# A two-stage Mamba scan: one softplus sum moved to TensorE, B and C spread by DMA, half-size dt transfers, and five products in 32 on GpSimd

## The chip, the cores and the metric

One core of a Trainium2 chip runs the whole program. The metric is the device time of one execution in microseconds, the median of three. Engines are named as the profile names them: PE (TensorE matmul), PEld (its weight load), DVE (VectorE), ACT (ScalarE), POOL (GpSimd) and SP (SyncE, which issues all DMAs here).

## The reference

The input is x of 64 channels, 256 time steps and 128 frequencies. Layer 0 runs a bidirectional Mamba block along time (128 sequences of length 256), adds a linear map of it, then does the same along frequency (256 sequences of length 128). Layer 1 is a small convolutional LSTM over 32 windows. Only layer 0 is touched. Cut to what matters, one direction of one Mamba block is:

```python
dt, Bm, Cm = jnp.split(jnp.einsum('nld,ed->nle', x, x_proj_w), [4, 20], axis=-1)
dt = jax.nn.softplus(jnp.einsum('nlr,dr->nld', dt, dt_proj_w) + dt_proj_b)
A = -jnp.exp(A_log)                                   # (128 channels, 16 states)
def step(h, inp):
    dt_t, B_t, C_t, x_t = inp
    h = jnp.exp(dt_t[:, :, None] * A) * h + dt_t[:, :, None] * B_t[:, None, :] * x_t[:, :, None]
    return h, jnp.einsum('nds,ns->nd', h, C_t)
```

So each of 128 channels carries 16 states. Per token there is a decay exp(dt*A), an input dt*x*B, a recurrence over the sequence, and a sum over the states weighted by C.

## The kernel before, in words

**Tiling.** A *stage* is one of the two Mamba passes (time, then frequency). A stage is cut into NCH = 64 *chunks* of 512 tokens, and a chunk has two directions. The 128 channels times 16 states of a direction are 2048 rows, that is sixteen tiles of 128 rows; they are worked as eight *pairs* of two tiles (128 x 1024 elements). A pair is numbered S: 16 pairs a chunk (8 forward, 8 backward), 1024 a stage, 2048 in all. `where(S)` gives chunk, direction d and the pair's place (k, r).

**The work of a pair.** `inputs` (L428) multiplies dtx = dt*x by a 0/1 selection matrix on TensorE, which spreads 8 channels over 128 rows and leaves the pair `bx` in PSUM (three buffers). `decays` has ACT compute exp(A*rep) into one of four `dA` buffers (L450), where `rep` is dt spread over the states: it is written to DRAM by `dt_away` (L384) and read back with a broadcast by `spread_dt` (L403), 1 MB for two pairs, three buffers. `times_b` multiplies bx by B on DVE (L462). `recur` is the scan on DVE (L472), which writes `h` (five buffers). `outputs` multiplies h by C on POOL (L485). `add_up` sums the states of two pairs back onto channels on TensorE (L500, with a first matmul L493).

**Swapped pairs.** For S % 32 in (5, 21, 29) the product with B is done by POOL instead (L459). The bx tile is first copied from PSUM to a dA buffer by ACT (L444), POOL multiplies there, ACT puts the decays into the PSUM tile, and the scan reads its two operands in exchanged places.

**The head of a chunk.** What a chunk needs ahead of its pairs is listed in HEAD: each entry is a slot and a name. Slot n of chunk c is done in step S = 16*(c-1)+n, so slots 0 to 15 run beside the pairs of the chunk before and slots 16 and up beside the chunk's own pairs. `project_x`, `project_z` and `silus` make xs and zs. `softplus_a` and `softplus_b` do relu, exp, log and two corrections on ACT; `softplus_c` and `softplus_d` add the four parts with three adds on POOL (L374, L375, L378); `times_x` makes dtx on POOL (L389). `project_bc` makes B or C, already spread over 128 rows, with one matmul (L395, weights repeated eight times) and one ACT copy (L397): four a chunk. All these matmuls share a single PSUM buffer (`ps_mm`, tag "mm"), so each waits until ACT has read the one before.

**What sets the order.** The whole layer runs under a manual schedule: every engine executes its instructions in program order. `run` writes, in each step S: the product with B for S+1, the scan of S, the gate (at S % 8 = 2), the product with C for S-1, bx for S+2, the decays of S+2, the HEAD entries of this step, then add_up for S-2 at odd S, and the closing matmuls at S % 16 = 2 and 3. SP issues DMAs in the same order; an issue that must wait holds up those behind it. In the order of instructions each DMA also waits for the eighth DMA before it (eight completion semaphores in turn).

Of the kernel before, what the change touches and what calls it, by code (L numbers as in the profile page):

```python
# [36 lines left out]
P = 128  # L37
# [9 lines left out]
NTOK = 512  # L47
# [8 lines left out]
FH = F // 2  # L56
HALF = T // 2
NRING = 4
NH = 5
LAG = 2  # L60
SWAPPED = (5, 21, 29)
EXP_AND_LN = "natural_log_exp_and_others"
SILU = "silu_and_others"
EDGES = (0, 1, LF - 2, LF - 1)
# [2 lines left out]

HEAD = (
    (-12, "load"),
    (-7, "squares"),  # L70
    (-6, "means"),
    (-6, "rms"),
    (-6, "normalise"),
    (0, "project_x", 0),
    (1, "project_z", 0),
    (4, "project_x", 1),
    (5, "project_z", 1),
    (5, "silus"),
    (7, "softplus_a", 0),
    (7, "softplus_b", 0),  # L80
    (9, "softplus_c", 0),
    (9, "project_bc", 0, 1),
    (10, "softplus_d", 0),
    (10, "dt_away", 0),
    (11, "softplus_a", 1),
    (11, "spread_dt", 0, 0),
    (12, "times_x", 0),
    (12, "project_bc", 1, 1),
    (12, "project_bc", 0, 0),
    (12, "spread_dt", 0, 1),  # L90
    (13, "softplus_b", 1),
    (13, "project_bc", 1, 0),
    (14, "spread_dt", 0, 2),
    (15, "softplus_c", 1),
    (16, "softplus_d", 1),
    (16, "spread_dt", 0, 3),
    (17, "dt_away", 1),
    (18, "spread_dt", 1, 0),
    (20, "times_x", 1),
    (20, "spread_dt", 1, 1),  # L100
    (22, "spread_dt", 1, 2),
    (24, "spread_dt", 1, 3),
)


class Mamba:


    def __init__(self, ctx, tc, d):
        nc = tc.nc  # L110
        self.nc, self.tc = nc, tc
        cp = ctx.enter_context(tc.tile_pool(name="m_const", bufs=1))
# [47 lines left out]
        nc.scalar.activation(self.A, self.A, AF.Exp)  # L160
        nc.vector.tensor_scalar(self.A, self.A, -1.0, None, ALU.mult)

        self.G1, self.G2, self.Wz, self.Wdt, self.Wb, self.Wc, self.Dd, self.W2 = ([] for _ in range(8))
        self.W3, self.lin_b = [], []
        with tc.tile_pool(name="m_prep", bufs=2) as pp, tc.tile_pool(
            name="m_prep_ps", bufs=2, space=PSUM
        ) as ps:
            lins = []
            for i, n in enumerate(("tlin", "flin")):
                lin = pp.tile([C, 2, C], F32, name=n, tag=n, bufs=1)  # L170
                nc.sync.dma_start(out=lin, in_=d[n + "_w"].rearrange("(h i) o -> i h o", h=2))
# [12 lines left out]
            for i in range(4):
                win = pp.tile([C, 2 * P], F32, name="win", tag="win")
                nc.sync.dma_start(out=win, in_=d["in_proj"][i])
                cw = pp.tile([C, 4, P], F32, name="cw", tag="cw")
                nc.sync.dma_start(out=cw, in_=d["conv_w"][i].partition_broadcast(C))
                xpd = pp.tile([RANK, P], F32, name="xpd", tag="xpd")
                nc.sync.dma_start(out=xpd, in_=d["x_proj_dt"][i])  # L190
                dtw = pp.tile([RANK, P], F32, name="dtw", tag="dtw")
                nc.sync.dma_start(out=dtw, in_=d["dt_proj"][i])
                xbc = pp.tile([P, NBC], F32, name="xbc", tag="xbc")
                nc.sync.dma_start(out=xbc, in_=d["x_proj_bc"][i])
                ow = pp.tile([C, P], F32, name="ow", tag="ow")
# [20 lines left out]
                for h, keep in ((0, self.Wb), (1, self.Wc)):  # L216
                    w = cp.tile([P, NS, DL], F32, name=f"wbc{h}{i}", tag=f"wbc{h}{i}")
                    nc.vector.tensor_copy(
                        w, xbc[:, h * NS : (h + 1) * NS].unsqueeze(2).to_broadcast([P, NS, DL])
                    )  # L220
                    keep.append(w.rearrange("p s d -> p (s d)"))
# [12 lines left out]
class Stage:  # L234
# [142 lines left out]
    def softplus_d(self, ch, d):  # L377
        self.nc.gpsimd.tensor_add(self.at["dt", d], self.at["lw", d], self.at["dt", d])  # L378

    def dt_away(self, ch, d):  # L380

        there = self.dram.tile([32, 4, NTOK], F32, name="there", tag="there")
        for r in range(4):
            self.nc.sync.dma_start(out=there[:, r], in_=self.at["dt", d][32 * r : 32 * r + 32])  # L384
        self.at["there", ch, d] = there

    def times_x(self, ch, d):
# [1 line left out]
        self.nc.gpsimd.tensor_mul(dtx, self.at["dt", d], self.at["xs", ch, d])  # L389
        self.at["dtx", ch, d] = dtx  # L390

    def project_bc(self, ch, d, h):
        wt = (self.m.Wb, self.m.Wc)[h][2 * self.stage + d]
        pb = self.mm("pb")
        self.nc.tensor.matmul(pb, lhsT=wt, rhs=self.at["xs", ch, d], start=True, stop=True)  # L395
        t = self.wk.tile([P, NTOK], F32, name="bc", tag=f"bc{h}", bufs=3)
        self.nc.scalar.copy(t, pb)  # L397
        self.at["BC"[h], ch, d] = t

    def spread_dt(self, ch, d, k):  # L400
        t = self.wk.tile([P, 4, NTOK], F32, name="rep", tag="rep", bufs=3)
        there = self.at["there", ch, d]
        self.nc.sync.dma_start(  # L403
            out=t, in_=there[DL * k : DL * (k + 1)].unsqueeze(0).to_broadcast([NS, DL, 4, NTOK])
        )
        self.at["rep", ch, d, k] = t

    def head(self, ch):
        todo = {}
# [20 lines left out]

    def swapped(self, S):

        return S % 32 in SWAPPED

    def decays(self, S):
        nc, m, L = self.nc, self.m, self.L
        ch, d, k, r = self.where(S)
        i = 2 * self.stage + d
        first, live = (0, slice(1, L)) if d == 0 else (L - 1, slice(0, L - 1))
        dA = self.dA[S % NRING]  # L440
        rep = self.at["rep", ch, d, k]
        if self.swapped(S):
            bx = self.at["bx", S]
            nc.scalar.copy(dA.rearrange("p j n l -> p j (n l)"), bx)  # L444
# [701 lines left out]
```

## Time and profile before

| what | before |
|---|---|
| time, median of 3 | 7585.94 us (7581.3 to 7589.56) |
| span of the profiled run | 7581.6 us |
| first scan starts, stage 0 | 75.7 us |
| gap between the last scan of stage 0 and the first of stage 1 | 3453 to 3509.6 us |
| last scan ends (layer 1 follows) | 6890 us |
| bytes of the SP queue | 1203 MB |
| rep<-there transfers, there<-dt, unp<-xn | 1024 of 1024 KB, 1024 of 64 KB, 512 of 64 KB |

The page gives busy time by engine for the whole run, but the run has three regimes: two scan stages that look alike and layer 1, whose 690 us are bounded by matmuls and are not touched. So a question on the scan is asked of a stretch inside a stage, for instance 1000 to 3000 us. The timeline lists instructions with start and duration; as an instruction's end overlaps the start of the next one on the same engine by some 0.1 us, the cost of one is read as the distance between two starts. In the list of waits, an engine's idle time is put down to what ended it.

### The profile page before, as it was taken

To read this page: it belongs to the slowest core of one execution; us is meant where nothing else is said; L and a number is where in the kernel's file an instruction comes from. 1 tells how busy PE (TensorE), PEld (TensorE's weight loads), DVE (VectorE), ACT (ScalarE), POOL (GpSimd) and SP (SyncE) were. 2 spreads that over 40 slices of the span, in tenths; PEclk is the share of its full clock that TensorE was granted. 3 is DMA by queue.
4 is the path that set the end of the run, shared out by engine and by line. 5 is a ranking of instruction groups with operands and counts; after the bars stand their busy time and mean duration, and the time that the engine had idled before them with its cause. 6 is when DMAs were issued, how large, how long until landed. Compare 5 with 4: busy or idle time off the path is not lost.

```text
span 7581.6 us, 83087 instructions
## 1 busy us (share of the span) xinstructions
PE 6523.0 (86%) x24588; PEld 2179.7 (29%) x24588; DVE 7263.6 (96%) x5008; ACT 5568.8 (73%) x10188; POOL 6916.1 (91%) x3860
## 2 busy tenths in 40 slices
PE   6888888888888888887988888888888888888999
PEld 2222222222222222221222222222222222225887
DVE  6999999999999999997999999999999999996887
ACT  5778777777777877775787877878778787774333
POOL 6999999999999999996999999999999999995554
PEclk9999999999999999998999999999999999999999
DMA  5777877777777777775778777777777777772000
GB/s 131 175 178 175 183 174 177 174 174 182 176 181 174 174 182 177 180 173 124 184 182 186 171 176 172 171 181 172 178 173 171 179 171 179 172 172 77 15 15 17
DMA packets 276049, 1208.67 MB, mean 159 GB/s; under 512 B 46704, under 2 KB 104720, under 8 KB 144528
## 3 DMA queue, kind: packets, MB, share of 16 engines
q1 hardware_dynamic: 275600, 1203.35, 68.9%
q8 instruction: 200, 3.28, 0.2%
q14 instruction: 249, 2.04, 0.1%
HBM read 1094.12 MB, written 75.50 MB: 154 GB/s over the span
## 4 chain that ended last, share of the span: by engine, by line
PE 21%; ACT 10%; issue 9%; DVE 6%; DMA 5%; POOL 4%; SPq 0%; POOLq 0%; DVEq 0%; ACTq 0%
PE cv L911 6%; DVE h L472 5%; PE bx L428 4%; DMA rep<-there 4%; ACT dA L450 3%; POOL h L485 3%; PE y L500 2%; PE pb L395 2%; DVE bx L462 1%; PE y L493 1%; ACT L342 1%; PE pg L967 1%; PE px L322 1%; ACT L347 1%; PE both L1023 1%
## 5 line engine op out<-in xcount | busy, mean ns | idle before, releaser
L485 POOL TENSOR_TENSOR h<-h,bc 128x1024 f32<-128x1024 f32 x2048 | 4806.7, 2365 | 179.0 <-DVE h L472 167.7
L472 DVE TENSOR_TENSOR_SCAN h<-dA,bx 128x1024 f32<-128x1024 f32 x1856 | 4205.5, 2275 | 0.7 <-POOL e L374 0.7
L428 PE MATMUL bx<-dtx,sel 64*128 64x512 f32 x8192 | 2371.3, 654 | 755.2 <-DVE h L472 736.0
L450 ACT ACTIVATE dA<-rep,A 128x510 f32<-128x510 f32 (+1 forms) x3712 | 2461.6, 713 | 453.7 <-DMA rep<-there 439.9
L462 DVE TENSOR_TENSOR bx<-bx,bc 128x1024 f32<-128x1024 f32 x1856 | 2245.9, 1210 | 117.0 <-PE bx L428 116.0
L428 PEld LDWEIGHTS bx<-dtx,sel 64*128 64x128 f32 x8192 | 648.2, 189 | 2390.1 <-issue 1093.5
L500 PE MATMUL y<-h,fold 128*32 128x512 f32 x8192 | 1272.4, 638 | 25.9 <-POOL h L485 22.9
L395 PE MATMUL pb<-xs,wbc 128*128 128x512 f32 x1024 | 655.8, 726 | 119.8 <-ACT bc L397 112.8
L444 ACT COPY dA<-bx 128x1024 f32<-128x1024 f32 x192 | 194.4, 1012 | 474.7 <-PE bx L428 472.4
L500 PEld LDWEIGHTS y<-h,fold 128*32 128x32 f32 x8192 | 185.6, 111 | 969.8 <-issue 455.2
L459 POOL TENSOR_TENSOR dA<-dA,bc 128x1024 f32<-128x1024 f32 x192 | 453.5, 2362 | 5.6 <-ACT dA L444 5.6
L397 ACT COPY bc<-pb 128x512 f32<-128x512 f32 x512 | 294.4, 575 | 218.2 <-PE pb L395 218.2
L472 DVE TENSOR_TENSOR_SCAN h<-bx,dA 128x1024 f32<-128x1024 f32 x192 | 438.4, 2283 | 12.6 <-POOL dA L459 10.8
L374 POOL TENSOR_TENSOR e<-e,w 128x512 f32<-128x512 f32 x256 | 327.1, 1278 | 68.8 <-ACT w L369 68.4
L375 POOL TENSOR_TENSOR lw<-lw,e 128x512 f32<-128x512 f32 x256 | 326.0, 1273 | 20.1
L389 POOL TENSOR_TENSOR dtx<-dt,xs 128x512 f32<-128x512 f32 x256 | 327.4, 1279 | 0.0
L378 POOL TENSOR_TENSOR dt<-lw,dt 128x512 f32<-128x512 f32 x256 | 326.6, 1276 | 0.3
L395 PEld LDWEIGHTS pb<-xs,wbc 128*128 128x128 f32 x1024 | 166.9, 205 | 554.3 <-ACT bc L397 318.9
L322 PE MATMUL px<-unp,g 128*128 128x512 f32 x512 | 291.4, 650 | 31.3 <-ACT X L544 17.8
L324 ACT ACTIVATE xs<-px,cb 128x512 f32<-128x512 f32 x256 | 175.4, 685 | 175.9 <-PE px L323 173.9
L355 PE MATMUL pv<-xs,wdt 128*128 128x512 f32 x512 | 294.1, 657 | 12.0 <-ACT xs L346 9.9
L329 PE MATMUL pz<-unp,wz 64*128 64x512 f32 x512 | 271.0, 609 | 9.0 <-ACT xs L324 8.8
(187 smaller groups left out, 6983.0 us busy)
## 6 DMA issues: line engine op xcount, KB each, us to landing
rep<-there SPq DMA_DIRECT2D x1024, 1024.0 KB
there<-dt SPq DMA_DIRECT2D x1024, 64.0 KB
unp<-xn SPq DMA_DIRECT2D x512, 64.0 KB
u<-in_x SPq DMA_DIRECT2D x128, 64.0 KB
out<-y SPq DMA_DIRECT2D x32, 256.0 KB
w<-in_W_ih_f SPq DMA_DIRECT2D x10, 512.0 KB
w<-in_W_ih_b SPq DMA_DIRECT2D x10, 512.0 KB
cw<-in_conv_w SPq DMA_DIRECT2D x4, 128.0 KB
```

The costliest lines, as they stand in the source:

```text
L322: nc.tensor.matmul(self.seqs(px), lhsT=m.G1[i], rhs=self.unp[:, :, first : first + L], start=True, stop=False)
L374: self.nc.gpsimd.tensor_add(e, e, w)
L389: self.nc.gpsimd.tensor_mul(dtx, self.at["dt", d], self.at["xs", ch, d])
L395: self.nc.tensor.matmul(pb, lhsT=wt, rhs=self.at["xs", ch, d], start=True, stop=True)
L428: self.nc.tensor.matmul(bx[:, j], lhsT=self.m.sel[rows, r, k], rhs=dtx[rows], start=True, stop=True)
L450: nc.scalar.activation(dA[:, j, :, live], self.seqs(rep[:, r + 2 * j])[:, :, live], AF.Exp, scale=m.A[:, i, g : g + 1])
L459: self.nc.gpsimd.tensor_mul(bx, bx, b)
L462: self.nc.vector.tensor_mul(bx, bx, b)
L472: self.nc.vector.tensor_tensor_scan(h.rearrange("p j n -> p (j n)")[:, step], dA[:, step], bx[:, step], 0.0, ALU.mult, ALU.add,)
L485: self.nc.gpsimd.tensor_mul(h, h, self.at["C", ch, d].unsqueeze(1).to_broadcast([P, 2, NTOK]))
L500: nc.tensor.matmul(y[32 * r : 32 * r + 32], lhsT=m.fold[:, k], rhs=hs[r % 2][:, r // 2], start=False, stop=k == NK - 1, skip_group_check=True,
L911: self.nc.tensor.matmul(t[:, g, :, 0:n_out], lhsT=wts[s][:, gate * P : (gate + 1) * P], rhs=self.parts[n][:, :, s : s + n_out], start=s == ...
```

## The change

- **Softplus of direction 0**: the four parts (relu, exp, correction, log) are summed by four matmuls with the identity into PSUM and one ACT copy, instead of three POOL adds. Direction 1 keeps the POOL adds.
- **B and C**: one matmul a direction gives all 32 rows (16 of B, 16 of C), ACT copies 32 x 512, the tile goes to DRAM, and two DMAs read it back spread over 128 rows. The wide weights wb and wc go away.
- **rep**: a transfer carries the dt rows of one pair (512 KB) instead of two; seven buffers of half the size instead of three. `there` is laid out so that the two rows of a pair are adjacent.
- **Swapped pairs**: S % 32 in (5, 10, 15, 21, 26), five in two chunks instead of three.
- **HEAD** is rearranged to go with this.

It is for taking work off DVE (products with B) while giving POOL room for it.

```diff
-SWAPPED = (5, 21, 29)
+NREP = 7
+SWAPPED = (5, 10, 15, 21, 26)
...
-    (7, "softplus_a", 0),
-    (7, "softplus_b", 0),
-    (9, "softplus_c", 0),
-    (9, "project_bc", 0, 1),
-    (10, "softplus_d", 0),
+    (7, "project_bc", 0),
+    (8, "softplus_a", 0),
+    (8, "softplus_b", 0),
+    (9, "spread_bc", 0, 0),
+    (9, "spread_bc", 0, 1),
+    (10, "softplus_sum", 0),
     (10, "dt_away", 0),
+    (10, "spread_dt", 0, 0),
+    (11, "times_x", 0),
+    (12, "project_bc", 1),
+    (13, "softplus_a", 1),
+    (14, "softplus_b", 1),
+    (15, "spread_dt", 0, 2),
...
+    def softplus_sum(self, ch, d):
+        nc = self.nc
+        ps = self.mm("ps")
+        parts = [self.at[n, d] for n in ("dt", "e", "w", "lw")]
+        for n, t in enumerate(parts):
+            nc.tensor.matmul(ps, lhsT=self.m.ident, rhs=t, start=n == 0, stop=n == len(parts) - 1)
+        nc.scalar.copy(self.at["dt", d], ps)
...
-    def project_bc(self, ch, d, h):
-        wt = (self.m.Wb, self.m.Wc)[h][2 * self.stage + d]
-        pb = self.mm("pb")
-        self.nc.tensor.matmul(pb, lhsT=wt, rhs=self.at["xs", ch, d], start=True, stop=True)
-        t = self.wk.tile([P, NTOK], F32, name="bc", tag=f"bc{h}", bufs=3)
+    def project_bc(self, ch, d):
+        pb = self.mm("pb")[0:NBC]
+        self.nc.tensor.matmul(pb, lhsT=self.m.Wbc[2 * self.stage + d], rhs=self.at["xs", ch, d], start=True, stop=True)
+        t = self.wk.tile([NBC, NTOK], F32, name="bc", tag="bc")
         self.nc.scalar.copy(t, pb)
+        away = self.dram.tile([NBC, NTOK], F32, name="away", tag="away")
+        self.nc.sync.dma_start(out=away, in_=t)
+
+    def spread_bc(self, ch, d, h):
+        t = self.wk.tile([P, NTOK], F32, name="BC"[h], tag="BC"[h], bufs=3)
+        self.nc.sync.dma_start(
+            out=t, in_=away[NS * h : NS * (h + 1)].unsqueeze(1).to_broadcast([NS, DL, NTOK])
+        )
...
-        t = self.wk.tile([P, 4, NTOK], F32, name="rep", tag="rep", bufs=3)
+        t = self.wk.tile([P, 2, NTOK], F32, name="rep", tag="rep", bufs=NREP)
-            out=t, in_=there[DL * k : DL * (k + 1)].unsqueeze(0).to_broadcast([NS, DL, 4, NTOK])
+            out=t, in_=there[DL * k : DL * (k + 1), r].unsqueeze(0).to_broadcast([NS, DL, 2, NTOK])
```

More of the change, by code (lines that the diff above doesn't have):

```diff
@@ L69 @@
     (-12, "load"),
[L70 to L73, printed above, removed]
+    (-8, "squares"),
+    (-5, "means"),
+    (-5, "rms"),
+    (-4, "normalise"),
     (0, "project_x", 0),
@@ L78 @@
     (5, "silus"),
-    (7, "softplus_a", 0),
-    (7, "softplus_b", 0),
-    (9, "softplus_c", 0),
-    (9, "project_bc", 0, 1),
-    (10, "softplus_d", 0),
-    (10, "dt_away", 0),
[L85 to L89, printed above, removed]
-    (12, "spread_dt", 0, 1),
[L91 to L96, printed above, removed]
+    (7, "project_bc", 0),
[4 more added lines that the diff above has]
+    (10, "softplus_sum", 0),
+    (10, "dt_away", 0),
+    (10, "spread_dt", 0, 0),
+    (11, "times_x", 0),
+    (12, "project_bc", 1),
+    (12, "spread_dt", 0, 1),
+    (13, "softplus_a", 1),
+    (14, "softplus_b", 1),
+    (15, "spread_dt", 0, 2),
+    (15, "spread_dt", 0, 3),
+    (15, "spread_dt", 0, 4),
+    (15, "spread_dt", 0, 5),
+    (16, "softplus_c", 1),
+    (17, "softplus_d", 1),
+    (17, "spread_dt", 0, 6),
     (17, "dt_away", 1),
-    (18, "spread_dt", 1, 0),
+    (18, "spread_dt", 0, 7),
+    (20, "spread_dt", 1, 0),
+    (20, "spread_bc", 1, 0),
     (20, "times_x", 1),
+    (20, "spread_bc", 1, 1),
     (20, "spread_dt", 1, 1),
-    (22, "spread_dt", 1, 2),
-    (24, "spread_dt", 1, 3),
+    (23, "spread_dt", 1, 2),
+    (23, "spread_dt", 1, 3),
+    (23, "spread_dt", 1, 4),
+    (25, "spread_dt", 1, 5),
+    (26, "spread_dt", 1, 6),
+    (26, "spread_dt", 1, 7),
 )
@@ L161, in __init__ @@
         nc.vector.tensor_scalar(self.A, self.A, -1.0, None, ALU.mult)
-        self.G1, self.G2, self.Wz, self.Wdt, self.Wb, self.Wc, self.Dd, self.W2 = ([] for _ in range(8))
+        self.G1, self.G2, self.Wz, self.Wdt, self.Wbc, self.Dd, self.W2 = ([] for _ in range(7))
         self.W3, self.lin_b = [], []
@@ L192, in __init__ @@
                 nc.sync.dma_start(out=dtw, in_=d["dt_proj"][i])
-                xbc = pp.tile([P, NBC], F32, name="xbc", tag="xbc")
+                xbc = cp.tile([P, NBC], F32, name=f"xbc{i}", tag=f"xbc{i}")
                 nc.sync.dma_start(out=xbc, in_=d["x_proj_bc"][i])
+                self.Wbc.append(xbc)
                 ow = pp.tile([C, P], F32, name="ow", tag="ow")
@@ L214, in __init__ @@
                 self.Wdt.append(wdt)
[L216 to L221, printed above, removed]
                 dd = cp.tile([P, P], F32, name=f"dd{i}", tag=f"dd{i}")
@@ L378, in softplus_d @@
         self.nc.gpsimd.tensor_add(self.at["dt", d], self.at["lw", d], self.at["dt", d])
+    def softplus_sum(self, ch, d):
[5 more added lines that the diff above has]
+        nc.scalar.copy(self.at["dt", d], ps)
     def dt_away(self, ch, d):
-        there = self.dram.tile([32, 4, NTOK], F32, name="there", tag="there")
+        there = self.dram.tile([32, 2, 2, NTOK], F32, name="there", tag="there")
         for r in range(4):
-            self.nc.sync.dma_start(out=there[:, r], in_=self.at["dt", d][32 * r : 32 * r + 32])
+            self.nc.sync.dma_start(out=there[:, r % 2, r // 2], in_=self.at["dt", d][32 * r : 32 * r + 32])
         self.at["there", ch, d] = there
@@ L390, in times_x, with spread_dt @@
         self.at["dtx", ch, d] = dtx
-    def project_bc(self, ch, d, h):
-        wt = (self.m.Wb, self.m.Wc)[h][2 * self.stage + d]
-        pb = self.mm("pb")
-        self.nc.tensor.matmul(pb, lhsT=wt, rhs=self.at["xs", ch, d], start=True, stop=True)
-        t = self.wk.tile([P, NTOK], F32, name="bc", tag=f"bc{h}", bufs=3)
-        self.nc.scalar.copy(t, pb)
+    def project_bc(self, ch, d):
+        pb = self.mm("pb")[0:NBC]
+        self.nc.tensor.matmul(pb, lhsT=self.m.Wbc[2 * self.stage + d], rhs=self.at["xs", ch, d], start=True, stop=True)
+        t = self.wk.tile([NBC, NTOK], F32, name="bc", tag="bc")
+        self.nc.scalar.copy(t, pb)
+        away = self.dram.tile([NBC, NTOK], F32, name="away", tag="away")
+        self.nc.sync.dma_start(out=away, in_=t)
+        self.at["away", ch, d] = away
+    def spread_bc(self, ch, d, h):
+        t = self.wk.tile([P, NTOK], F32, name="BC"[h], tag="BC"[h], bufs=3)
+        away = self.at["away", ch, d]
+        self.nc.sync.dma_start(
+            out=t, in_=away[NS * h : NS * (h + 1)].unsqueeze(1).to_broadcast([NS, DL, NTOK])
+        )
         self.at["BC"[h], ch, d] = t
-    def spread_dt(self, ch, d, k):
-        t = self.wk.tile([P, 4, NTOK], F32, name="rep", tag="rep", bufs=3)
+    def spread_dt(self, ch, d, n):
+        k, r = divmod(n, 2)
+        t = self.wk.tile([P, 2, NTOK], F32, name="rep", tag="rep", bufs=NREP)
         there = self.at["there", ch, d]
         self.nc.sync.dma_start(
-            out=t, in_=there[DL * k : DL * (k + 1)].unsqueeze(0).to_broadcast([NS, DL, 4, NTOK])
+            out=t, in_=there[DL * k : DL * (k + 1), r].unsqueeze(0).to_broadcast([NS, DL, 2, NTOK])
         )
-        self.at["rep", ch, d, k] = t
+        self.at["rep", ch, d, n] = t
     def head(self, ch):
@@ L440, in decays @@
         dA = self.dA[S % NRING]
-        rep = self.at["rep", ch, d, k]
+        rep = self.at["rep", ch, d, 2 * k + r]
         if self.swapped(S):
@@ L450, in decays @@
             nc.scalar.activation(
-                dA[:, j, :, live], self.seqs(rep[:, r + 2 * j])[:, :, live], AF.Exp, scale=m.A[:, i, g : g + 1]
+                dA[:, j, :, live], self.seqs(rep[:, j])[:, :, live], AF.Exp, scale=m.A[:, i, g : g + 1]
             )
```

## The prediction

> **What bounds the kernel now.** I read, in this order, busy time by stage, the groups, DVE's timeline, DVE's waits, PE's timeline and the DMA queues. First the stretch from 1000 to 3000 us inside stage 0 (columns: length, then busy us and count of PE, PEld, DVE, ACT, POOL, then clock, DMA share, GB/s):
>
> ```profile
> 1000.00:3000.00 2000.00, 1713.98 (x6298) 465.68 (x6294) 1992.54 (x1234) 1563.84 (x2808) 1947.06 (x1006) 0.98 0.77 177
> ```
>
> DVE works 99.6% of the stage, POOL 97%. The groups say what on:
>
> ```profile
> L485 POOL TENSOR_TENSOR h<-h,bc 128x1024 f32<-128x1024 f32 x2048 | 4806.7, 2365 | 179.0 <-DVE h L472 167.7
> L472 DVE TENSOR_TENSOR_SCAN h<-dA,bx 128x1024 f32<-128x1024 f32 x1856 | 4205.5, 2275 | 0.7 <-POOL e L374 0.7
> L462 DVE TENSOR_TENSOR bx<-bx,bc 128x1024 f32<-128x1024 f32 x1856 | 2245.9, 1210 | 117.0 <-PE bx L428 116.0
> L459 POOL TENSOR_TENSOR dA<-dA,bc 128x1024 f32<-128x1024 f32 x192 | 453.5, 2362 | 5.6 <-ACT dA L444 5.6
> L395 PE MATMUL pb<-xs,wbc 128*128 128x512 f32 x1024 | 655.8, 726 | 119.8 <-ACT bc L397 112.8
> ```
>
> DVE's timeline gives the true spacing:
>
> ```profile
> 1500.46 2.28 DVE L472 TENSOR_TENSOR_SCAN h<-dA,bx 128x1024 f32<-128x1024 f32 x1
> 1502.65 1.21 DVE L462 TENSOR_TENSOR bx<-bx,bc 128x1024 f32<-128x1024 f32 x1
> 1503.77 2.28 DVE L472 TENSOR_TENSOR_SCAN h<-dA,bx 128x1024 f32<-128x1024 f32 x1
> ...
> 1512.58 0.67 DVE L511 TENSOR_TENSOR yz<-y,zs 128x512 f32<-128x512 f32 x1
> 1513.16 1.23 DVE L462 TENSOR_TENSOR bx<-bx,bc 128x1024 f32<-128x1024 f32 x1
> ```
>
> A scan takes 2.19 us, a product 1.12, a gate 0.58. Two chunks (32 pairs, 3 swapped) are 29 x 1.12 + 32 x 2.19 + 4 x 0.58 = 104.9 us. Stage 0 lasts from 75.7 to 3453 us, 3377 / 32 = 105.5. So the stage is DVE's own work end to end; its waits from 200 to 3440 us are only
>
> ```profile
> DVE bx L462 <- PE bx L428: 7.8, 16, 0.9
> DVE h L472 <- POOL dA L459: 5.0, 22, 0.5
> ```
>
> (us in total, times, longest). The 116 us of the group are mostly the two starts of stages. ACT's 440 us for rep never reach DVE.
>
> **What the skill says.** The Trainium skill, "TensorE: Matmul & The Clock Gate", Part 1, says that PE's clock falls to half after an idle window of about 3.4 us and comes back after a busy one. The trace agrees; PE a little before a chunk's end:
>
> ```profile
> 1538.19 1.01 PE L297 MATMUL pm<-sq,ones 128*128 128x256 f32 x2 [1.62 <-ACT sq L292]
> 1539.13 2.08 PE L428 MATMUL bx<-dtx,sel 64*128 64x512 f32 x4
> ...
> 1544.38 1.13 PE L428 MATMUL bx<-dtx,sel 64*128 64x512 f32 x4
> 1545.44 1.13 PE L395 MATMUL pb<-xs,wbc 128*128 128x512 f32 x2
> 1547.36 1.12 PE L395 MATMUL pb<-xs,wbc 128*128 128x512 f32 x2 [0.79 <-ACT bc L397]
> ```
>
> bx takes 2.08 instead of 1.13 after idle time. A clock of 0.98 in the stage means half speed for 4% of it, about one such window in 80 us. "DMA: Bandwidth & Descriptors", Anatomy of one DMA, gives about 2.0 us fixed a DMA, mostly the receipt: the first 1 MB rep takes 6.9 us from issue (65.8) to its reader (72.7), against 4.55 us of transfer (below), so 2.3. The same page, Rules for kernel authors, wants an outermost dimension of a multiple of 16 to use all 16 engines: rep, B and C all have 16 outermost. "Trainium Kernel Development and Optimization", Key Constraints: GpSimd cannot access PSUM. Hence a swapped pair's copy (L444, 1.01 us on ACT).
>
> **DVE.** Two more swapped pairs in 32 remove two products: 2 x 1.12 = 2.24 us of 104.9, over 64 double chunks **143 us**. Nothing is added to DVE.
>
> **POOL.** By starts: a big product 2.32 us, the three softplus adds 3.80, dtx 1.22, xn 0.70. Two chunks before: 35 x 2.32 + 4 x 5.02 + 2 x 0.70 = 102.7. After: 37 x 2.32 + 2 x 5.02 + 2 x 1.22 + 1.4 = 99.7, against DVE's 102.7. The even chunk (pairs 5, 10, 15 swapped) has 51.0 of POOL against 50.8 of DVE, the odd one 48.7 against 51.9, so I followed the backlog step by step: a swapped step brings POOL 4.64 us while DVE passes in 2.19; later steps win back about 1.0 each. Backlog is highest, 4.4 us, in step 4 (with dtx of direction 1), and falls to 0.4 or less before pairs 10 and 15. A swapped product stands behind outputs(S-3) and has 6.6 - 4.7 = 1.9 us to spare when POOL is caught up, so the scan does not wait. With h in five buffers, 4.4 us do not stop the scan either.
>
> **PE.** An identity matmul has the form of L355 or L395, 1.06 us (2.08 cold). Four are 4.2 us, in two chunks +8.5; half of the eight L395 matmuls go, -4.2. PE's distances sum to 86.6 us in two chunks before, 90.9 of 102.7 after: 88%. But the four come in one block at step 10 with bx(13) queued behind, for which DVE waits. Step 10 starts when scan 9 ends, call it 0. bx(12) ends at 1.2, the block at 5.4, bx(13) at 6.5; DVE wants it at 7.2 (two steps and a gate). Then pm 0.7, L493 1.0 and y 1.0 put bx(14) at 9.2 to 10.25, wanted at 10.5. So the worst slack is 0.25 us at full clock. Its inputs: w leaves ACT 7.5 us after step 8 starts, 2.0 after step 10 does, and w is the third operand, wanted at 3.3. The old wait, L395 for L397 (113 us), shrinks as there is one pb in a step instead of two or three.
>
> **ACT.** Four bc copies of 0.48 a chunk become two of no more, and one of 0.59 for the sum; two more swapped copies with their zeroing in two chunks are +2.4 us. ACT is at 78% of the stage: hidden behind DVE. Its block at step 8 (copy and decays of pair 10, six softplus instructions of 3.65 us) leaves the decays of pair 11 ready about 1.2 us before scan 11.
>
> **DMA.** 1203 MB take 68.9% of 16 engines over 7581.6 us:
>
> ```profile
> q1 hardware_dynamic: 275600, 1203.35, 68.9%
> ```
>
> that is 4.34 us a MB, so 1 MiB of rep 4.55 and 512 KB 2.28. A chunk has about 9.2 MB or 40 us; B and C add 4 x 0.26 MB and `away` 0.13: 5.1 us, so 45 of 51.4 us, 88%. Seven half buffers free one by one: rep n+7 may start seven steps (22 us) before its use, where before three buffers gave five (16.5). rep(0,0) leaves about 10 us after step 8's softplus and is there some 4 us before its scan's decays must start. B lands before step 15 by more than 10 us. The eight semaphores allow eight DMAs in flight; as SP only waits for its own oldest, no DMA that I followed is late. Hidden, by DVE. Unknown is a 4 KB piece against the 8 KB one: equal bytes a second (284 ns each) from below, while the queue binds from about 340 ns.
>
> **Starts of stages.** PE is cold there and idle before, DVE waits for all of it. In stage 1 before, relu is there at 3488.6 and w at 3491.2, dt at 3495.2, scan 0 starts at 3509.6. After, the softplus starts 2.9 us later (pb is ahead of pv in the single PSUM buffer), and four cold matmuls (2 us each) and a copy end at about 3500, +4.9; the half-size rep gives back 2.3, and B and C no longer stand in the way. I take +1.5 a stage, **+3** (0 to +6).
>
> **Sum.** 7586 - 143 + 3 = 7446 without new waits. For PE's thin slack I add waits: half-clock windows come about once a chunk now; where one falls on step 6 to 7 (bx alone) or before px, bx comes 1 to 1.5 us late. Taking that for one chunk in six, 21 x 1.2 = **25**: 7471. Low end: no such waits and some of the present ones gone, 7435.
>
> **Rivals.**
> (a) The block is late by 0.6 us in every chunk, as ACT's w or the 0.25 us of slack fails: 7446 + 128 x 0.6 = 7523, still faster. For it: the slack. Against it: ACT has 1.2 us to spare.
> (b) A PE wait takes the place of the product: 1.1 us a chunk, +141, 7587, no change.
> (c) The block itself runs at half clock in every other chunk: 8.3 instead of 4.2 us, less the 0.25, is 3.85 x 64 = 246, so 7692, slower than before. For it: the half-clock bx above stands just at steps 10 to 11. Against it: that window came from PE idling for 1.6 and more before pm; after, step 9 is short and the PE is over 60% busy in steps 8 and 9.
> A DMA piece of 360 ns would give 46 + 8 = 54 us a chunk and about 7740; I count it with (c). The page's whole queue shows no sign of a price by the piece that would do it.
>
> **How the numbers follow.** Expected case 0.66, 7471; (a) 0.17, 7523; (b) 0.05, 7587; (c) with the DMA case 0.12, 7692. The range takes the first two: 7435 to 7545. Faster 0.84, same 0.04, slower 0.12.
>
> **What would show it.** Right: the product on DVE x1728 and DVE still at 99% of 1000 to 3000; stage 0 at about 103 us per 32 pairs; POOL at 97%; PE's wait for bc nearly gone; DMA share 0.85 to 0.9. Wrong: DVE waiting for bx (L428) by tens of us in a stage at steps 11 to 13, bx behind ps of over 2 us, or DVE's scan waiting for dA behind rep, B or C.

## The result, and the profile after

The changed kernel takes **7402.22 us** (7401.08 to 7409.75, four runs), the kernel before 7585.49 beside it: a ratio of 0.976, 95% interval 0.9744 to 0.9777. That is 183 us less. I had predicted 115 less, 7471 with a range of 7435 to 7545: the direction was right, the gain was more than half as large again as I had it, and the time lies below the range.

First the stage, 1000 to 3000 us of the kernel after (length; then busy us and count of PE, PEld, DVE, ACT, POOL; clock, DMA share, GB/s):

```profile
1000.00:3000.00 2000.00, 1760.05 (x6623) 495.21 (x6620) 1998.94 (x1228) 1625.41 (x2919) 1944.81 (x955) 0.99 0.82 205
```

DVE rose from 1992.54 to 1998.94: the 7.5 us in 2000 that it still lost before are down to 1.1. POOL is at 97% as before, PE is at 88%, and the granted clock rose from 0.98 to 0.99. Then the groups of the page after (count, total busy us, mean ns, idle time just before and what ended it), which answer to the five shown of before:

```profile
L510 POOL TENSOR_TENSOR h<-h,C 128x1024 f32<-128x1024 f32 x2048 | 4809.9, 2368 | 149.6 <-DVE h L497 128.3
L497 DVE TENSOR_TENSOR_SCAN h<-dA,bx 128x1024 f32<-128x1024 f32 x1728 | 3900.4, 2273 | 3.0 <-ACT dA L475 2.6
L487 DVE TENSOR_TENSOR bx<-bx,B 128x1024 f32<-128x1024 f32 x1728 | 2097.1, 1214 | 99.6 <-PE bx L452 98.9
L484 POOL TENSOR_TENSOR dA<-dA,B 128x1024 f32<-128x1024 f32 x320 | 756.8, 2365 | 35.4 <-ACT dA L469 31.2
L359 PE MATMUL pv<-xs,wdt 128*128 128x512 f32 x512 | 290.5, 650 | 118.0 <-ACT bc L410 118.0
```

128 products went from DVE (1856 to 1728) to POOL (192 to 320), at unchanged duration each. PE's old wait for the bc copy is not gone: it has moved to pv, which now stands behind pb in the single PSUM buffer. Nothing on DVE waits for it. Almost all of DVE's 99.6 us for bx lie at the two starts of stages; from 200 to 3350 us, the whole list of DVE's waits is one line (us in all, times, longest):

```profile
DVE bx L487 <- PE bx L452: 1.3, 3, 0.4
```

Before, two lines stood there, with 7.8 and 5.0 us. And the DMA queue carries more bytes in a hardly larger share of a shorter span:

```profile
q1 hardware_dynamic: 509072, 1354.46, 73.1%
```

**Where 181 us of span went** (7581.6 to 7401.0), from the starts of the scans in both traces:

| part | before | after | difference |
|---|---|---|---|
| first scan starts | 75.7 | 73.8 | -1.9 |
| stage 0, first to last scan | 3377.4 | 3286.7 | -90.7 |
| last scan of stage 0 to first of stage 1 | 56.4 | 53.0 | -3.5 |
| stage 1, first to last scan | 3380.5 | 3292.7 | -87.9 |
| after the last scan (layer 1) | 691.6 | 694.9 | +3.3 |

The two stages give 178.5 us. The two removed products are 64 x 2 x 1.12 = 143 of them. The other 35 are waits that DVE had before and has no more: without any wait, 32 pairs take 104.9 us before and 102.63 after, and both stages together stood 45.5 us above 64 times that figure before, and 11 after.

What those waits were is seen in DVE's timeline of the kernel before, at pair 29 (start, duration; in brackets the idle time and its releaser), and POOL's product of the same pair:

```profile
1756.43 1.21 DVE L462 TENSOR_TENSOR bx<-bx,bc 128x1024 f32<-128x1024 f32 x1
1757.84 2.29 DVE L472 TENSOR_TENSOR_SCAN h<-bx,dA 128x1024 f32<-128x1024 f32 x1 [0.20 <-POOL dA L459]
```

```profile
1755.44 2.36 POOL L459 TENSOR_TENSOR dA<-dA,bc 128x1024 f32<-128x1024 f32 x1
```

POOL's product for the swapped pair ends at 1757.80, 0.2 us after DVE would have gone on. The scan of pair 29 is late by 0.28 us in the median, once in every two chunks; over both stages that sums to some 21 us, and another 15 us come from bx standing behind the matmuls of pb at steps 12 and 13. After, at a swapped pair the scan follows the product at once:

```profile
1663.50 1.21 DVE L487 TENSOR_TENSOR bx<-bx,B 128x1024 f32<-128x1024 f32 x1
1664.62 2.28 DVE L497 TENSOR_TENSOR_SCAN h<-bx,dA 128x1024 f32<-128x1024 f32 x1
```

The start of a stage is the other surprise. Before, PE (columns as above) around the first product on DVE:

```profile
63.44 2.08 PE L395 MATMUL pb<-xs,wbc 128*128 128x512 f32 x2 [1.42 <-ACT dt L359]
...
68.94 2.07 PE L395 MATMUL pb<-xs,wbc 128*128 128x512 f32 x2 [0.68 <-ACT bc L397]
70.94 4.40 PE L428 MATMUL bx<-dtx,sel 64*128 64x512 f32 x12
```

```profile
73.12 1.23 DVE L462 TENSOR_TENSOR bx<-bx,bc 128x1024 f32<-128x1024 f32 x1 [45.42 <-PE bx L428]
```

DVE's first product waited for bx behind three cold matmuls of pb (at half clock, 2.07 us each), each with its copy on ACT: 63.4 to 70.9 us. The first scan follows the second product, also late for bx; rep, which I had followed, was with ACT at 72.68, so that the decays alone (1.33 us) would have let the scan start at some 74.0. In the kernel after the block of four stands on PE ahead of that, 57.88 to 64.5, bx is there before the decays, and what the scan waits for is rep and then the decays on ACT:

```profile
57.88 2.08 PE L390 MATMUL ps<-dt,ident 128*128 128x512 f32 x2 [1.36 <-ACT dt L363]
...
63.17 1.37 PE L390 MATMUL ps<-lw,ident 128*128 128x512 f32 x2
```

```profile
72.42 1.33 ACT L475 ACTIVATE dA<-rep,A 128x510 f32<-128x510 f32 x2 [1.14 <-DMA rep<-there]
```

```profile
73.78 2.29 DVE L497 TENSOR_TENSOR_SCAN h<-dA,bx 128x1024 f32<-128x1024 f32 x1 [0.94 <-ACT dA L475]
```

### The profile page after: what moved, and what is told of

Its sections match the earlier page's. It is cut to its first block, busy times and chain, and to the rows that moved or that the text cites. A ratio compares the mean times of both kernels' runs of the same rounds, so it can differ in the third digit from the quotient of the medians.

```text
span 7401.0 us, 86351 instructions
## 1 busy us (share of the span) xinstructions
PE 6514.6 (88%) x25100; PEld 2231.0 (30%) x25100; DVE 7106.8 (96%) x4872; ACT 5632.0 (76%) x10316; POOL 6735.3 (91%) x3604
## 3 DMA queue, kind: packets, MB, share of 16 engines
q1 hardware_dynamic: 509072, 1354.46, 73.1%
## 4 chain that ended last, share of the span: by engine, by line
PE 19%; ACT 12%; issue 10%; DVE 10%; DMA 3%; POOL 1%; SPq 0%; DVEq 0%; POOLq 0%; ACTq 0%
DVE h L497 7%; PE cv L936 6%; PE bx L452 3%; ACT dA L475 3%; PE y L525 2%; DMA rep<-there 2%; DVE bx L487 2%; PE px L326 1%; ACT bx L475 1%; ACT L351 1%; ACT L346 1%; PE px L327 1%; ACT xs L350 1%; ACT dA L469 1%; PE y L518 1%
## 5 line engine op out<-in xcount | busy, mean ns | idle before, releaser
L510 POOL TENSOR_TENSOR h<-h,C 128x1024 f32<-128x1024 f32 x2048 | 4809.9, 2368 | 149.6 <-DVE h L497 128.3
L497 DVE TENSOR_TENSOR_SCAN h<-dA,bx 128x1024 f32<-128x1024 f32 x1728 | 3900.4, 2273 | 3.0 <-ACT dA L475 2.6
L475 ACT ACTIVATE dA<-rep,A 128x510 f32<-128x510 f32 (+1 forms) x3456 | 2277.9, 711 | 180.0 <-DMA rep<-there 166.7
L487 DVE TENSOR_TENSOR bx<-bx,B 128x1024 f32<-128x1024 f32 x1728 | 2097.1, 1214 | 99.6 <-PE bx L452 98.9
L484 POOL TENSOR_TENSOR dA<-dA,B 128x1024 f32<-128x1024 f32 x320 | 756.8, 2365 | 35.4 <-ACT dA L469 31.2
L497 DVE TENSOR_TENSOR_SCAN h<-bx,dA 128x1024 f32<-128x1024 f32 x320 | 729.1, 2279 | 0.0
L475 ACT ACTIVATE bx<-rep,A 128x510 f32<-128x510 f32 (+1 forms) x640 | 441.0, 689 | 21.2 <-ACT bx L472 0.4
L326 PE MATMUL px<-unp,g 128*128 128x512 f32 x512 | 298.4, 665 | 42.1 <-DMA unp<-xn 22.8
L408 PE MATMUL pb<-xs,xbc 128*32 128x512 f32 x512 | 269.4, 608 | 8.0 <-ACT xs L350 6.4
L518 PE MATMUL y<-xs,dd 128*128 128x512 f32 x512 | 275.2, 619 | 0.0
L327 PE MATMUL px<-unp,g 128*128 128x512 f32 x512 | 270.0, 609 | 0.0
```

Of the source, the lines that this page charges most:

```text
L326: nc.tensor.matmul(self.seqs(px), lhsT=m.G1[i], rhs=self.unp[:, :, first : first + L], start=True, stop=False)
L327: nc.tensor.matmul(self.seqs(px), lhsT=m.G2[i], rhs=self.unp[:, :, second : second + L], start=False, stop=True)
L475: nc.scalar.activation(dA[:, j, :, live], self.seqs(rep[:, j])[:, :, live], AF.Exp, scale=m.A[:, i, g : g + 1])
L484: self.nc.gpsimd.tensor_mul(bx, bx, b)
L487: self.nc.vector.tensor_mul(bx, bx, b)
L497: self.nc.vector.tensor_tensor_scan(h.rearrange("p j n -> p (j n)")[:, step], dA[:, step], bx[:, step], 0.0, ALU.mult, ALU.add,)
```

## The experiments

Each result stands as the time, with the ratio to the kernel before on the same chip and its 95% interval. "Floor" means DVE's own work without waits. The diffs are cut to the lines that tell the change; "..." marks a cut inside one.

### The count and the places of swapped pairs, in the new kernel

If the gain beyond 143 us comes from waits that are gone, they should stay gone when the products are put back, and each product should be worth 64 x 1.12 = 72 us. First the three places of before:

```diff
-SWAPPED = (5, 10, 15, 21, 26)
+SWAPPED = (5, 21, 29)
```

> The changed kernel with the three swapped pairs of before (5, 21, 29): 29 products in 32 on DVE again, all else as changed. Theory 1 (the two products are 2 x 1.13 us of DVE in 32 pairs, 144 us in all, and the rest of the gain is waits that the rearranged head took away): 7402 + 144 = 7546, with 32 pairs at 104.9 us. Theory 2 (the waits belong to the place of the third pair, 29): its wait of 0.36 us comes back, 64 x 0.36 = 23 more, 7569. Theory 3 (all of the gain is the products): back at 7585.

Measured 7566.13 (0.997, 0.9958 to 0.9982). The value is that of the second theory, but not its cause: the wait is on bx, not on the swapped product. PE's timeline at step 28 (the same place in the chunk as step 12), and then DVE's:

```profile
1740.26 1.13 PE L452 MATMUL bx<-dtx,sel 64*128 64x512 f32 x4 [1.18 <-DVE h L497]
1741.32 1.12 PE L390 MATMUL ps<-dt,ident 128*128 128x512 f32 x2
1742.28 1.02 PE L390 MATMUL ps<-e,ident 128*128 128x512 f32 x2
1743.14 1.02 PE L390 MATMUL ps<-w,ident 128*128 128x512 f32 x2
1744.00 1.02 PE L390 MATMUL ps<-lw,ident 128*128 128x512 f32 x2
1744.95 1.13 PE L452 MATMUL bx<-dtx,sel 64*128 64x512 f32 x4
1746.01 0.70 PE L301 MATMUL pm<-sq,ones 128*128 128x256 f32 x2
1746.55 1.02 PE L518 MATMUL y<-xs,dd 128*128 128x512 f32 x2
1747.50 1.07 PE L525 MATMUL y<-h,fold 128*32 128x512 f32 x8
1748.49 1.13 PE L452 MATMUL bx<-dtx,sel 64*128 64x512 f32 x4
```

```profile
1749.67 1.23 DVE L487 TENSOR_TENSOR bx<-bx,B 128x1024 f32<-128x1024 f32 x1 [0.16 <-PE bx L452]
```

This is the thin place that the prediction worked out: the block of four, bx, pm, two matmuls for y, bx. The block takes 1741.32 to 1744.95, 3.6 us, not the 4.2 of four times 1.06, as matmuls that go on in one sum start 0.86 to 0.96 us apart. With pair 29 swapped, DVE passes a step without a product just there, is 1.12 us earlier, and waits; with the five places of the kernel after it does not, and has about 0.8 us to spare where I had 0.25.

So I took places that leave that step its product, and then other counts:

```diff
-SWAPPED = (5, 10, 15, 21, 26)
+SWAPPED = (5, 21, 26)
```

> The changed kernel with three swapped pairs at 5, 21 and 26; against the run with 5, 21 and 29 only the place of one differs. Theory 1 (with 29, bx of pair 30 comes 0.24 us late behind the block of the sum, as DVE passes step 28 without a product): the wait goes, 7566 - 20 = 7546. Rival (the place makes no difference): 7566.

Measured 7540.02 (0.9941, 0.9926 to 0.9956), as the sum had it. Its stage is at DVE's floor:

```profile
1000.00:3000.00 2000.00, 1731.46 (x6479) 485.60 (x6481) 1998.84 (x1240) 1544.76 (x2786) 1820.73 (x896) 0.98 0.80 201
```

It does as many products on each engine as the kernel before, and is 45 us faster. **So about 45 of the 183 us have nothing to do with the two products: they are waits and starts.**

```diff
-SWAPPED = (5, 10, 15, 21, 26)
+SWAPPED = (5, 10, 21, 26)
```

> The changed kernel with four swapped pairs, 5, 10, 21 and 26. Theory 1 (one product is worth its own time on DVE, 64 x 1.13 = 72 us, as long as POOL has room): 7402 + 72 = 7474, half of the way from five to three at places without a wait. Rival (the places 5, 10, 15, 21, 26 only work together): waits of DVE on top, 7490 or more.

Measured 7468.11 (0.9848, 0.9831 to 0.9865), again as expected. Last, one more:

```diff
-SWAPPED = (5, 10, 15, 21, 26)
+SWAPPED = (5, 10, 15, 21, 26, 31)
```

> The changed kernel with a sixth swapped pair, 31. DVE 101.5 us in 32 pairs, POOL 39 x 2.32 + 12.5 + 1.4 = 104.4. Theory 1 (POOL is full and becomes the bound): 102.6 -> 104.4, +115, 7517, slower than five. Rival (DVE stays the bound): 7402 - 72 = 7330.

Measured **7378.7** (0.9731, 0.9717 to 0.9746), faster than both kernels, 23.5 us under the kernel after. My expectation of POOL was slipped by one: 32 products with C and 6 swapped ones are 38 x 2.32, which makes 102.0 us of POOL in 32 pairs, not 104.4, against 101.5 of DVE. POOL then bounds, with 0.6 us per 32 pairs less than DVE's 102.63 before this step: 38 us for the run, of which 24 came. Its stage shows two engines full:

```profile
1000.00:3000.00 2000.00, 1817.61 (x6664) 498.94 (x6662) 1991.86 (x1215) 1658.29 (x2973) 1995.19 (x980) 1.00 0.83 206
```

From three to six pairs the time goes 7540, 7468, 7402, 7379: gains of 72, 66 and 24. The product on DVE is worth its own duration until POOL is full.

### The five pairs, or new places, in the kernel before

```diff
-SWAPPED = (5, 21, 29)
+SWAPPED = (5, 10, 15, 21, 26)
```

> The kernel before with the five swapped pairs alone; POOL keeps all softplus adds. Theory 1 (POOL then has 37 x 2.32 + 4 x 5.02 + 1.4 = 107.3 us of work in 32 pairs against 102.6 on DVE, so POOL becomes the bound): 64 x (107.3 - 105.5) = +115, near 7700, slower. Rival (DVE stays the bound): 7585 - 144 = 7441.

Measured 8263.19 (1.089, 1.0871 to 1.0908): far over both theories. The stage shows that POOL's sum of work alone is not the reason:

```profile
1000.00:3000.00 2000.00, 1663.70 (x5730) 447.40 (x5728) 1789.79 (x1087) 1462.21 (x2616) 1847.26 (x949) 0.93 0.71 162
```

POOL is busy 92%, DVE 89%, and no engine is full. The waits of the same stretch:

```profile
PE y L500 <- POOL h L485: 83.4, 50, 3.6
POOL dA L459 <- ACT dA L444: 143.4, 45, 5.2
DVE h L472 <- POOL dA L459: 116.3, 51, 3.5
```

POOL's idle time is almost all for ACT's copies of swapped pairs, and by the timeline it lies before the products of pair 10 (4.3 us in every 32 pairs) and pair 26 (3.2). There the copy follows at once on the last of the softplus instructions (L369): ACT is not waiting for bx, it is busy with what stands ahead. POOL, once late, is late for the sums on PE and for DVE's scans. The excess is largest at scans 10, 15 and 26. Is it the places or the number? Two runs with three pairs:

```diff
-SWAPPED = (5, 21, 29)
+SWAPPED = (5, 15, 21)
```

> The kernel before with its third swapped pair moved from 29 to 15, still three. Theory 1 (in the trace of before, scan 29 comes 0.36 us late in every 32 pairs as POOL's product for it is late behind the adds of steps 9 to 12, 23 us in all; scan 31 waits for bx as the PE has pb, pb, pv and pb in steps 12 and 13, 15 us, and this stays): 7585 - 23 = 7562. Rival (the late scan comes from the head of the chunk and not from the place): no change, 7585.

Measured 7601.33 (1.002, 1.0013 to 1.0027). The wait at 29 is gone, and scan 15 is 0.3 us late instead: bx(16) stands behind the pb matmuls. Neither theory: the wait moves with the pair, and the run is 14 us slower than the kernel before on the same chip.

```diff
-SWAPPED = (5, 21, 29)
+SWAPPED = (5, 21, 26)
```

> The kernel before with its third swapped pair moved from 29 to 26, still three; nothing else. With the new head the same three places ran at 7540, 45 us under before. Theory 1 (the place is good only with the new head: in the old one POOL has its softplus adds in steps 25 and 26, ahead of the product of pair 26, and pb stands in steps 28 and 29 all the same): the waits move and do not go, 7585 or slower. Rival (the place alone gives the gain): 7540 to 7560.

Measured 7913.32 (1.0432, 1.0414 to 1.0449). The same three places take 7540 under the new head: place alone is not it, the head is. What ACT does ahead of pair 26's copy in the old head:

```profile
1818.49 0.63 ACT L369 ACTIVATE w<-w 128x512 f32<-128x512 f32 x1
1819.03 0.99 ACT L444 COPY dA<-bx 128x1024 f32<-128x1024 f32 x1
```

```profile
1820.10 2.35 POOL L459 TENSOR_TENSOR dA<-dA,bc 128x1024 f32<-128x1024 f32 x1 [3.39 <-ACT dA L444]
```

```profile
1822.48 2.29 DVE L472 TENSOR_TENSOR_SCAN h<-bx,dA 128x1024 f32<-128x1024 f32 x1 [1.69 <-POOL dA L459]
```

The six softplus instructions of slot 7 (1815.38 to 1819.03) stand on ACT before the copy, POOL idles 3.39 us for it, the scan 1.69. The new head has them in slot 8, behind the copy and the decays of pairs 10 and 26. The trace makes that move, one changed digit in two lines of the diff, the likely reason why places 10 and 26 are usable in the new head; no run made it alone. Nor does it account for all of the loss: of the 5.4 us that DVE is idle in 32 pairs, 1.9 are at scan 26, and most of the rest are waits for bx at the pairs that follow, which were not followed further back.

### The softplus sum

Back on POOL in the kernel after:

```diff
-    (10, "softplus_sum", 0),
+    (9, "softplus_c", 0),
+    (10, "softplus_d", 0),
```

> The changed kernel with the softplus of direction 0 added on POOL again, as before (adds in steps 9 and 10), no sum on PE; five swapped pairs. Theory 1 (POOL has 107.3 us of work in 32 pairs and becomes the bound): 7402 + 64 x (107.3 - 102.7) = 7696, with DVE idle for about 4.5% of a stage, and the PE, without its block of four matmuls, falls to half clock more often than the 49 times of the changed kernel. Rival (POOL's backlog is absorbed by the h buffers): within 20 us of 7402.

Measured 7801.32 (1.0282, 1.0267 to 1.0297). POOL is full, as expected, and 32 pairs take 109.1 us against 107.3 of POOL's own work:

```profile
1000.00:3000.00 2000.00, 1685.48 (x5950) 446.35 (x5952) 1900.17 (x1158) 1516.85 (x2712) 1965.25 (x1009) 0.95 0.77 193
```

The rest over the expected 7696 is time in which POOL itself stands idle, 1.9 us in 32 pairs, most of it for ACT's w and for a copy (17.8 and 6.7 us in this stretch). PE waits 128.5 us for h from POOL (PE y L526), with bx behind, as it must behind a full POOL. PE has 150 windows at half clock, against 49 in the kernel after, as expected. So the sum on PE is what pays for the two products. Alone, in the kernel before:

```diff
-    (9, "softplus_c", 0),
-    (10, "softplus_d", 0),
+    (10, "softplus_sum", 0),
```

> The kernel before with one part of the change: the softplus of direction 0 summed by four matmuls at step 10; three swapped pairs (5, 21, 29), old B and C, old rep, old places. Theory 1 (scan 29 waits 0.25 to 0.36 us in every 32 pairs since POOL's product is late behind the softplus adds): POOL falls to 95.1 us, that wait goes (-23), but bx comes late behind the block and pb at steps 11 to 13, 0.3 us a chunk (+38): 7600. Rival (the PE takes the block without a wait): 7562.

Measured 7994.29 (1.0546, 1.053 to 1.0563), 400 us over the expected. Two waits of 1000 to 3000 us carry it:

```profile
POOL xn L307 <- ACT rs L302: 217.3, 36, 7.6
DVE bx L470 <- PE bx L436: 115.2, 93, 3.4
```

In the old head the normalisation of the next chunk (slot -6, step 10) shares the step with the sum: ACT's rs stands behind the copy of ps, POOL's xn waits about 6 us for it in each chunk, with the products with C behind; and pb at step 12 has bx behind it. The change moves the normalisation to slots -5 and -4; that move alone was not tried. I had costed the whole rearrangement of the head at nothing.

### B and C, and the rep transfers, put back

Old wide matmuls for B and C in the kernel after, in the old slots:

```diff
-    (7, "project_bc", 0),
-    (9, "spread_bc", 0, 0),
-    (9, "spread_bc", 0, 1),
+    (9, "project_bc", 0, 1),
...
-    (12, "project_bc", 1),
+    (12, "project_bc", 1, 1),
+    (12, "project_bc", 0, 0),
+    (13, "project_bc", 1, 0),
```

> The changed kernel with B and C made as before: four wide matmuls a chunk (steps 9, 12, 12, 13) and four 128x512 copies through the one PSUM buffer, no spread from DRAM. Theory 1 (the spread from DRAM is what frees PE for the block of the sum): PE has 95 us of 102.6 in 32 pairs and two pb with an ACT copy between them behind the block, so DVE waits for bx at steps 12 to 14, about 1 us a chunk: 7402 + 128 = 7530. Rival (PE has room for both): within 15 us of 7402.

Measured 8360.58 (1.1032, 1.101 to 1.1053), against some 7530 expected. From 1000 to 3000 us DVE waits 188.3 us for bx; PE's pb waits 93.1 us for ACT to read pv out of the one PSUM buffer, as ACT is at the copy and the decays of pair 15 there. So I brought them to where the new head has pb:

```diff
-    (7, "project_bc", 0),
+    (7, "project_bc", 0, 0),
+    (7, "project_bc", 0, 1),
...
-    (12, "project_bc", 1),
+    (12, "project_bc", 1, 0),
+    (12, "project_bc", 1, 1),
```

> The changed kernel with B and C from four wide matmuls and copies a chunk, as in the earlier run with old B and C, but at places where no pb stands behind a softplus matmul in the one PSUM buffer: two at step 7, two at step 12. Theory 1 (the 950 us of that run came from pb waiting for ACT to read pv): most of it goes; PE has 95 of 102.6 us and two pb with a copy between them cost DVE about 0.5 us a chunk, 7402 + 64 = 7466. Rival (PE has no room for the block and four pb): 7550 or more.

Measured 8176.74 (1.0782, 1.0766 to 1.0798), still far over. PE, then ACT, at step 7:

```profile
1530.62 1.13 PE L412 MATMUL pb<-xs,wbc 128*128 128x512 f32 x2
1535.14 1.23 PE L412 MATMUL pb<-xs,wbc 128*128 128x512 f32 x2 [3.39 <-ACT bc L414]
```

```profile
1531.89 1.28 ACT L355 ACT_TABLE_LOAD   x1
...
1534.52 0.56 ACT L414 COPY bc<-pb 128x512 f32<-128x512 f32 x1
```

The second pb waits 3.39 us for ACT's copy of the first, which stands behind the silus, the second of their two table loads of 1.28 us and the decays of a pair; y and bx stand behind the second pb on PE, and the scan that follows, which needs an h buffer that y has yet to read, comes 2.32 us late. Of the 10.8 us that DVE is idle in 32 pairs, 9.1 are at scans 9 to 11 of the two chunks. The new head has a single pb there, and the next use of the buffer is pv. **What B and C by DMA buy here is less the time of two matmuls than one handover of the PSUM buffer less in a step.** That the price is this large was in neither theory. Whether the four wide matmuls have places in which they cost less was not tried further.

Old 1 MB transfers of rep with three buffers, in the kernel after:

```diff
-        t = self.wk.tile([P, 2, NTOK], F32, name="rep", tag="rep", bufs=NREP)
+        t = self.wk.tile([P, 4, NTOK], F32, name="rep", tag="rep", bufs=3)
```

with the old layout of `there` and the old slots of spread_dt.

> The changed kernel with the dt rows sent as before: 1 MB for two pairs, three buffers, old slots. Theory 1 (no wait of DVE came from rep before, and DVE hides the transfers): the first rep of a stage is 2.3 us longer, 7402 + 5 = 7407, and ACT waits for rep some 400 us instead of 167. Rival (ACT, held up by rep, is late with the copies of the five swapped pairs): DVE waits of 0.5 us a chunk or more, 7466 or slower.

Measured 7622.68 (1.0051, 1.0036 to 1.0066), 220 us over the kernel after. The time is that of the second theory (over 7466), but not its cause: ACT's wait for rep is hardly longer than in the kernel after (62.0 against 56.8 us from 1000 to 3000 us), and the wait that counts is another:

```profile
PE px L318 <- DMA unp<-xn: 63.9, 34, 4.0
DVE bx L478 <- PE bx L443: 52.2, 46, 4.5
```

SP's queue at such a place:

```profile
1498.10 0.52 SPq L418 DMA_DIRECT2D rep<-there  x1
1500.25 0.30 SPq L404 DMA_DIRECT2D away<-bc  x1
1500.59 0.52 SPq L418 DMA_DIRECT2D rep<-there  x1
1501.22 2.46 SPq L307 DMA_DIRECT2D unp<-xn  x4
```

The small unp transfers, which the next chunk's matmuls wait for, are issued behind 2 MB of rep. The last of them is issued by 1503.68; PE has it at 1511.36:

```profile
1511.36 1.10 PE L318 MATMUL px<-unp,g 128*128 128x512 f32 x2 [2.37 <-DMA unp<-xn]
```

The Trainium skill, "DMA: Bandwidth & Descriptors", Queues, rings and completion order, says that each DMA engine takes the descriptors of a ring in order; PE's 63.9 us for unp agree with that. To part this from the size itself, the second rep was issued one step later, behind unp:

```diff
-    (12, "spread_dt", 0, 1),
+    (13, "spread_dt", 0, 1),
```

> The changed kernel with 1 MB dt transfers in three buffers, as in the run with the old rep, but the second transfer of a chunk issued one step later (13), behind the four unp transfers and not ahead of them. Theory 1 (in that run unp stood behind 2 MB of rep, 9.1 us, in the DMA queue, so px and with it bx were late): px no longer waits for unp and the time falls from 7623 to 7430 or less. Rival (three buffers of two pairs free too late for this head): it stays above 7550.

Measured 7529.97 (0.9925, 0.9911 to 0.994), between the two theories. The wait for unp is gone from the list and 93 of the 220 us with it; 128 stay, with these lines:

```profile
ACT dA L466 <- DMA rep<-there: 149.7, 119, 3.3
POOL dA L475 <- ACT dA L460: 43.3, 43, 3.1
DVE bx L478 <- PE bx L443: 27.1, 26, 2.1
```

I read them so: ACT is late at the decays as rep is late, then late at the copies of swapped pairs, and with five swapped pairs that reaches DVE. In the kernel before ACT waited for rep as well (440 us in the run, 492 in this one) and it reached no one; in the kernel after that wait is 167 us. That the two further copies make the difference is not shown: no run had the 1 MB transfers with three swapped pairs under the new head.

## Why the prediction was wrong

**DVE's sum: right.** Two products of 1.12 us in 32 pairs, 143 us; the floor of 102.63 us per 32 pairs is what the scans show nearly everywhere. Removing them one at a time gave 72 and 66 us. The product counts 1728.

**POOL and PE's budget: right.** 99.7 us of 102.7 worked out for POOL, 97.2% measured (PE 88% and 88%), and no scan waits for the swapped products. What I did not see is how much of that rests on ACT: the backlog was followed on POOL alone, taking the copy as ready. Under the old head it is not (pair 26: 3.39 us).

**PE's thin slack, +25: failed.** This is the first of the two steps that put the time out of the range. Two terms in it were mis-sized. The block takes 3.6 us, not 4.2, since I took the spacing of separate matmuls for matmuls of one sum. And I priced a half-clock window that meets a bx at 1.2 us of DVE's time, in one chunk of six. That cost did not come: the run with places 5, 21 and 26 has 98 windows at half clock in the trace's clock records, nearly as many as the 116 before, and DVE waits in it no more than in the kernel after with 49 (1.3 us from 200 to 3350 us in both). Inside the stages, away from their starts, 81 of 91 windows of the kernel before start in steps 8 to 10 of a chunk; in that run 72 of 75 start in steps 14 and 15, and in the kernel after 33 of 37. In that run the bx of the next pairs (0, 1, 16, 17) is ready some 1.9 us before DVE comes to it, in the median, and a bx at half clock takes 0.95 us more (2.08 for 1.13).

Why the windows fell from 116 to 49 has two parts. The block lies in the idle time of steps 8 to 10: with it one window is left there, and with the adds back on POOL (a run that also stalls elsewhere) 64 are there again. But with the block and three swapped pairs there are still 98 (5, 21, 26) or 74 (5, 21, 29), with four 88, with five 49, with six 32: between a third and three quarters of the fall come only with the two further swapped pairs, which make a chunk shorter, so that PE is busy for more of the time. The Trainium skill, "TensorE: Matmul & The Clock Gate", Part 1, gives the window as about 3.4 us; here 87 of the 116 last 3.41 us and nearly all others a multiple of that. Its rule that the clock falls after an idle window, for which the prediction found agreement, is not what this trace shows as it stands: before a fall in the stages PE was busy for 38% of the 3.41 us ahead, in the median, and its longest idle stretch there was 2.1 us (1.62 in the lines that the prediction shows).

**Present waits: left in.** The second failed step. I read 7.8 and 5.0 us off the list of DVE's waits and left them in the sum unchanged. That list was of stage 0 alone (stage 1 has 10.0 and 5.7), and it counts idle time from the end of the instruction before, which overlaps the next start by 0.1 us, so a scan that comes 0.3 us late stands in it with 0.2. And the sum beside it (105.5 against 104.9 us per 32 pairs) already said that more was lost. The starts of scans put it at 45.5 us over both stages, of which 34.5 went: pair 29's late product, and bx behind two or three pb at steps 12 and 13. I had halved the pb matmuls in PE's budget without asking which DVE wait they made. I put this gain at the low end of the range only.

**Starts of stages, +3: failed in sign.** -1.9 and -3.5 us, -5.4 in all. The block delays the softplus by less than the 4.9 us that I had: in stage 0 the first rep is issued 2.05 us later (67.81 for 65.76). The half-size rep gives back its 2.3 (with its reader 4.6 us after the issue instead of 6.9), which leaves 0.26 us gained. What I left out is that bx stood behind three cold pb matmuls and set the first scan; the other 1.6 us are that wait, which is gone.

**After the last scan, +3.3,** was not in the prediction and is not explained. It does not belong to the new head: from the end of the last scan the traces of all kernels take 691.5 to 695.8 us, those with the new head 692 to 696, those with the old 691.5 to 694.

Together: 25 that did not come, 34.5 that went, 8.4 at the starts, less 3.3 is 64.6. The span fell by 180.6 where I had 115, a miss of 65.6; the remaining 1 us is rounding.

**DMA: right, with a margin.** 88% was the sum, 82% came. The trace's pieces of 4 KB take 259 ns on average, those of 8 KB 578, so half-size pieces were a little cheaper per byte and the feared 360 ns did not appear. The size is the reason, as far as the runs go: with the 1 MB transfers under the new head the 8 KB pieces took 572 and 576. The page's 2.0 us fixed a DMA, which the prediction cites, are given there for transfers issued by GpSimd, and these are issued by SP; the 2.3 us beside them is an estimate from this trace, and nothing in the sum rests on either.

**The rivals.** (a), a late block in each chunk, is the wait of the run with places 5, 21 and 29 (0.3 us per 32 pairs), but only there. (b) and (c) did not come about: 1.3 us of waits for bx leave room for neither. PE's wait for bc did not go away, as I had said, but moved to pv, where it costs nothing.

What stays open: which single edit of the head took away which of the 35 us. Each of the three parts (sum, B and C, rep) undone alone cost 130 to 960 us, and the two that were done alone in the kernel before (five pairs, sum) cost 400 us and more, so their prices can't be added, and the 35 us can't be read from them. A sum on PE for both directions was not tried.

## What to carry to other kernels

A sum of work per engine tells which engine can bound, and here it told the gain of a moved instruction to within 10% (72 and 66 us for 72) as long as the order of the others holds; it says nothing of an order that does not hold, where kernels with no engine above 93% lost 8 to 10%. Before costing an edit, compare the measured distance of the bottleneck's instructions with its sum of work: the difference is waits that the edit may remove, and each has a name. And when an edit moves entries of a hand-written order, ask for each engine what now stands ahead of the instruction that others wait for: in the runs of 7913, 7994 and 8177 us the traces point to a softplus one step too early, a normalisation one step too early and one PSUM handover too many.

## What the runs showed of the hardware that was not expected

- Matmuls of 128x512 f32 start 1.06 us apart when separate, 0.86 to 0.96 when they add into one PSUM sum.
- Four added matmuls a chunk did not lower PE's clock: the windows at half clock left the steps where the block stands, and their number went from 116 to 98 with three swapped pairs (5, 21, 26), 49 with five and 32 with six, with PE busy for 1731, 1760 and 1818 of the 2000 us in 1000 to 3000. The mean clock there was 0.98, 0.99 and 1.00.
- The clock fell to half after 3.41 us in which PE was busy for 38% of the time in the median and never idle for more than 3.1 us at a stretch (kernel before, 110 falls in the stages).
- DRAM rows read sixteen times over into 128 partitions: 4 KB pieces 259 ns, 8 KB pieces 578 ns; the queue as a whole took 3.99 us a MB after (73.1% of 7401 us for 1354 MB) and 4.34 before.
- 64 KB transfers issued behind two of 1 MB on the same queue held PE for up to 4.0 us; issued ahead of the second, they held it no more.
